# The row of s_dst: from four TensorE transposes and a ScalarE copy to a VectorE transpose and two transfers through a DRAM line

One core of a Trainium2 chip. The metric is device time in microseconds, the median of the runs of one kernel.

## The reference, cut to what matters

64 graphs of 256 nodes and 128 features go through four layers, each followed by a residual sum and a layer norm. Layer 0 is a gated recurrence of five steps. Layer 2 contains the graph attention that the change concerns:

```python
h = x @ Wp + bp
s_src = (h * a_src).sum(-1); s_dst = (h * a_dst).sum(-1)
scores = s_src[:, :, None] + s_dst[:, None, :]           # row of s_dst beside column of s_src
scores = where(scores >= 0, scores, 0.2 * scores)
attn = softmax(where(A <= 0, -inf, scores), axis=-1)
h_gat = (attn * A) @ h                                   # then layer norm, relu, a GIN layer
```

The matmul gives `s_dst` as a column (a node per partition). The scores need it as a row that every partition holds.

## The kernel before: the parts that matter

Two graphs make a pair; 32 pairs go through. A small list scheduler in the kernel places every operation of every pair in the instruction lists of five engines, from costs and latencies that it is told. `N_PAIR` limits how many pairs are in flight. The last three pairs (the tail) use a variant of the code with more TensorE transposes.

```python
N_PAIR = 8
LATENCY = {PE: 230, ACT: 80, DVE: 80, POOL: 120, SP: 1800}
# ...
ts = bank()                                               # a PSUM bank
def f():
    for c in range(C):                                    # C = 4 in a full-width pair
        nc.tensor.transpose(ts.ap[:, c * P:(c + 1) * P],
                            h2.ap[:, c, D + 1:D + 2].to_broadcast([P, P]), ident.ap)
# ... full-width pairs (29 of 32):
add(PE, 112 * C, f, [h2, ident], [ts], [ts, sd, u, mx, nm, rd])
add(ACT, act(C * P) - 45, lambda: nc.scalar.copy(sd.ap.rearrange(...), ts.ap.rearrange(...)), [ts], [sd])
# ... then on VectorE, at its place in that engine's list:
nc.vector.tensor_tensor_reduce(out=uc(c), in0=sd.ap[:, b * N:(b + 1) * N], in1=mask.ap[:, it, :], ...)
```

The column, repeated along the free dimension, is transposed against the identity: every partition of the bank gets the row. After the mask operation come leaky ReLU and exponential on ScalarE, a product and a block transpose on VectorE, four transfers of `wT`, and the weighted matmul on TensorE (L809).

A step of layer 0 is a chain as well: matmuls, tanh on ScalarE, three VectorE operations, a VectorE block transpose to `S`, four transfers of `htok`, and the next step's mixing matmul (L533), its copy and the next matmuls.

Of the kernel before, what the change touches and what calls it, by code (L numbers as in the profile page):

```python
# [7 lines left out]
F32 = mybir.dt.float32  # L8
# [4 lines left out]
P = 128  # L13
N = 256
D = 128
# [6 lines left out]
N_T = 58  # L22
N_W = 6
N_H = 6
N_PAIR = 8
N_TAIL = 3

MATS = ["w3a", "w3b", "w4a", "w4b", "w5a", "w5b", "u3", "u5",
# [11 lines left out]
PE, ACT, DVE, POOL, SP = range(5)  # L40
LATENCY = {PE: 230, ACT: 80, DVE: 80, POOL: 120, SP: 1800}


def place(p):

    return 20000 * min(p, 27) + 6000 * max(p - 27, 0)


class Buf:


    def __init__(self, tag, slots, make):
        self.tag, self.slots, self.make = tag, slots, make
        self.ap, self.slot, self.left, self.writer, self.readers = None, None, 0, [], []


class Op:
    def __init__(self, eng, cost, fn, rank, takes):
        self.eng, self.cost, self.fn, self.rank, self.takes = eng, cost, fn, rank, takes
        self.uses, self.before, self.n_before, self.ready = [], [], 0, 0  # L60


class Graph:
# [3 lines left out]
    def add(self, eng, cost, fn, rank, reads=(), writes=(), takes=()):  # L67
        op = Op(eng, cost, fn, rank, takes)
        deps = set()
        for b in reads:  # L70
            deps.update(b.writer)
            b.readers.append(op)
        for b in writes:
            deps.update(b.writer)
            deps.update(b.readers)
            b.writer, b.readers = [op], []
        for b in takes:
            b.writer = b.writer or [op]
        for b in {id(b): b for b in (*reads, *writes, *takes)}.values():
            b.left += 1  # L80
            op.uses.append(b)
        deps.discard(op)
        for d in deps:
            d.before.append(op)
        op.n_before = len(deps)
        self.ops.append(op)
        return op

    def order(self):
        clock = [0] * 5  # L90
        free = {}
        for op in self.ops:
            for b in op.takes:
                free.setdefault(b.tag, [(0, i) for i in range(b.slots)])
        waiting = [[] for _ in range(5)]
        for op in self.ops:
            if not op.n_before:
                waiting[op.eng].append(op)

        for op in reversed(self.ops):  # L100
            op.tail = op.cost + max((n.tail + (LATENCY[op.eng] if n.eng != op.eng or op.eng != PE else 0)
                                     for n in op.before), default=0)
        for op in self.ops:
            op.rank = (place(op.rank[0]) - op.tail, op.rank)
        out = []
        self.busy = [0] * 5
        while len(out) < len(self.ops):
            best = None
            for e in range(5):
                pick = None  # L110
                for op in waiting[e]:
                    at = max(op.ready, clock[e])
                    need = {}
                    for b in op.takes:
                        need[b.tag] = need.get(b.tag, 0) + 1
                    for tag, n in need.items():
                        if len(free[tag]) < n:
                            at = None
                            break
                        at = max(at, free[tag][n - 1][0])  # L120
                    if at is None:
                        continue
                    key = (at, op.rank)
                    if pick is None or key < pick[0]:
                        pick = (key, op)
                if pick is not None and (best is None or pick[0] < best[0]):
                    best = pick
            (at, _), op = best
            waiting[op.eng].remove(op)
            for b in op.takes:  # L130
                b.slot = free[b.tag].pop(0)[1]
            clock[op.eng] = at + op.cost
            self.busy[op.eng] += op.cost
            end = at + op.cost + LATENCY[op.eng]
            op.start = at
            for b in op.uses:
                b.left -= 1
                if b.left == 0 and b.slots:
                    free[b.tag].append((end, b.slot))
                    free[b.tag].sort()  # L140
            for n in op.before:
                n.n_before -= 1
                n.ready = max(n.ready, end if n.eng != op.eng or op.eng != PE else at + op.cost)
                if not n.n_before:
                    waiting[n.eng].append(n)
            out.append(op)
        self.end = max(clock)
        return out
# [9 lines left out]
def kernel(ctx: ExitStack, tc: tile.TileContext, xT, xs, adjs, mats, cols, rows, out):  # L158
    nc = tc.nc
    NPAIR = xT.shape[0]  # L160

    const = ctx.enter_context(tc.tile_pool(name="const", bufs=1))
    work = ctx.enter_context(tc.tile_pool(name="work", bufs=1))
    psum = ctx.enter_context(tc.tile_pool(name="psum", bufs=1, space=bass.MemoryType.PSUM))
    ctx.enter_context(tc.manual_schedule())
    g = Graph()

    def fixed(shape, name):
        b = Buf(name, 0, None)
        b.ap = const.tile(shape, F32, name=name)  # L170
        return b

    def temp(shape, tag, slots, name=None):
        return Buf(tag, slots, lambda i: work.tile(shape, F32, tag=f"{tag}{i}", name=name or tag))

    def flat(name):
        return temp([P, 512], "t", N_T, name)

    def wide(name):
        return temp([P, 4, D], "t", N_T, name)  # L180
# [7 lines left out]
    def bank():  # L188
        return Buf("ps", 8, lambda i: psum.tile([P, 512], F32, tag=f"ps{i}", name="ps"))


    diff, ident = fixed([P, P], "diff"), fixed([P, P], "ident")
    A = {n: fixed([P, 2, N], n) for n in ADJS[:-1]}
    aTs, a_s, aTss = A["aTs"], A["as"], A["aTss"]
# [27 lines left out]
    HT, XS = [flat("hT") for _ in range(NPAIR)], [wide("xs") for _ in range(NPAIR)]  # L222
    token = [Buf("pair", N_PAIR, lambda i: None) for _ in range(NPAIR)]

# [200 lines left out]
    maskb, ginT = fixed([P, 2, N], "maskb"), fixed([P, 2, N], "ginT")  # L425
# [50 lines left out]
    maskn, wpxn, vxn = fixed([P, 2, N], "maskn"), fixed([P, HW], "wpxn"), fixed([P, 2, D], "vxn")  # L476
# [42 lines left out]
    def build(p):  # L519
        n = [0]  # L520

        def add(eng, cost, fn, reads=(), writes=(), takes=()):
            n[0] += 1
            g.add(eng, cost, fn, (p, n[0]), reads, writes, takes)

        def mix(src, m):

# [48 lines left out]
        if p < NPAIR - N_TAIL:  # L576
            layers123(p, add, x_t, x0, (0, 1), False)
        else:
            for b in range(2):
                layers123(p, add, x_t, x0, (b,), True)  # L580

    def layers123(p, add, h, x0, bs, by_pe):

        nb = len(bs)
        C = 2 * nb
# [5 lines left out]
        def act(n, aps=0):  # L591
            return 250 + 0.745 * n + 93 * aps

        def wide(name):
            return temp([P, C, D], "t", N_T, name)

        def flat(name):
            return temp([P, C * P], "t", N_T, name)
# [118 lines left out]
        def f():  # L717
            for it in range(2):
                o, i = (b.ap.rearrange("p (b t) d -> p b t d", t=2)[:, :, it, :] for b in (xd, x_t))
                nc.scalar.activation(o, i, AF.Copy, scale=dcol.ap[:, it:it + 1])  # L720
# [13 lines left out]
        h2 = temp([P, C, HW], "h2", N_H, "h2")  # L734
# [9 lines left out]
                h2.ap[:, 2 * b:2 * b + 2, :], th.ap[:, :2 * HW].rearrange("p (t d) -> p t d", d=HW),  # L744
                hbias.ap[:, None, :].to_broadcast([P, 2, HW])), [th, hbias], [h2])

        ts = bank()

        def f():
            for c in range(C):  # L750
                nc.tensor.transpose(ts.ap[:, c * P:(c + 1) * P], h2.ap[:, c, D + 1:D + 2].to_broadcast([P, P]), ident.ap)  # L751
        u = temp([P, C * N], "w", N_W, "u") if nb == 2 else temp([P, C * N], "t", N_T, "u")
        mx, nm, rd = (temp([P, C], k, 6) for k in ("mx", "nm", "rd"))
        if by_pe:
            add(PE, 112 * C, f, [h2, ident], [ts], [ts, u, mx, nm, rd])
            sd, mask, edges = ts, maskn, A["ass"]
        else:
            sd, mask, edges = flat("sd"), maskb, a_s
            add(PE, 112 * C, f, [h2, ident], [ts], [ts, sd, u, mx, nm, rd])
            add(ACT, act(C * P) - 45, lambda: nc.scalar.copy(sd.ap.rearrange("p (c x s) -> p c x s", x=4, s=32),  # L760
                                                             ts.ap.rearrange("p (c s x) -> p c x s", x=4, s=32)),
                [ts], [sd])

        def uc(c):
            return u.ap[:, c * N:(c + 1) * N]
# [74 lines left out]
        R, o = temp([P, 2, nb, D], "t", N_T, "R"), wide("o")  # L840
        tt = [bank() for _ in range(nb)]
        v = vxn if by_pe else vx
# [96 lines left out]
```

## Time and profile before

| | before |
|---|---|
| time, median of 3 runs | 1566.67 us (1566.57 to 1567.11) |
| span of the profiled run | 1564.1 us |
| TensorE busy | 1538.2 us, 98% |
| period of a pair in the middle | 47.15 us |
| TensorE idle: first 50 us / middle / last 114 us | 6.1 / 1.8 / 18.0 us |

TensorE's records overlap, so their durations don't add up (at 593.30 us of the trace before, a group of four transposes is recorded as 0.60 us and the next matmul starts 0.44 us after it). I count as time on TensorE the distance from one start to the next. I use two figures of a trace throughout. **Work** is the count of TensorE records by form, times the median start-to-start time of that form in the trace before (429 ns for 512 columns, 216 for 256, 112 for 128 and for a transpose). **Rest** is the span less the work: waits, start and end. Before: 1564.1 = 1525.7 + 38.4.

### The profile page before, as it was taken

What the parts mean: (1) busy time and instruction counts of PE and PEld (TensorE: products, weight loads), DVE (VectorE), ACT (ScalarE), POOL (GpSimd) and SP (SyncE); (2) the same over time, 40 slices, a digit from 0 to 9 for tenths busy, and PEclk for the clock granted to TensorE, in tenths of its full rate; (3) what the DMA queues carried; (4) which work ended last, traced back from release to release, by engine and by line L of the source; (5) the groups of instructions that cost most, each with busy time, mean ns of one, the idle gap of its engine ahead of it and who ended that gap; (6) DMA issues with size and microseconds to landing.
All of it is one profiled execution on the core that took longest, in us unless ns stands there. A gap on an engine that the chain in (4) does not pass through costs nothing.

```text
span 1564.1 us, 21663 instructions
## 1 busy us (share of the span) xinstructions
PE 1538.2 (98%) x6480; PEld 1072.5 (69%) x6480; DVE 1100.4 (70%) x2550; ACT 992.3 (63%) x2227; POOL 459.5 (29%) x532
## 2 busy tenths in 40 slices
PE   8999999999999999999999999999999999999797
PEld 5556667776776676776676777666776676766686
DVE  4688787677666677666677666677666677867775
ACT  3345676666666666666676666676666667766663
POOL 0001233232333332322322333322232323323564
PEclk9999999999999999999999999999999999999998
DMA  6223454454444554444554444544445544535210
GB/s 217 43 36 54 63 75 76 75 92 77 74 68 73 90 88 75 80 65 74 93 85 74 78 69 74 95 80 77 79 70 75 95 72 84 91 53 80 40 21 28
DMA packets 719220, 117.67 MB, mean 75 GB/s; under 512 B 705408, under 2 KB 706176, under 8 KB 718976
## 3 DMA queue, kind: packets, MB, share of 16 engines
q1 hardware_dynamic: 718816, 115.76, 44.6%
q8 instruction: 53, 0.87, 0.2%
q14 instruction: 63, 0.52, 0.1%
q10 hardware_dynamic: 288, 0.53, 0.1%
HBM read 20.26 MB, written 8.39 MB: 18 GB/s over the span
## 4 chain that ended last, share of the span: by engine, by line
PE 94%; DVE 2%; POOL 1%; DMA 1%; SPq 1%; issue 0%; ACT 0%; POOLq 0%; DVEq 0%
PE ps L533 17%; PE ps L630 10%; PE ps L547 9%; PE ps L565 8%; PE ps L550 8%; PE ps L555 8%; PE ps L563 8%; PE ps L643 7%; PE ps L858 7%; PE ps L809 4%; PE ps L870 3%; PE ps L741 2%; PE ps L751 1%; SPq L514 1%; POOL rs L695 0%
## 5 line engine op out<-in xcount | busy, mean ns | idle before, releaser
L533 PE MATMUL ps<-aTs,htok 128*128 128x256 f32 x1024 | 241.5, 379 | 0.2 <-DMA htok<-S 0.2
L533 PEld LDWEIGHTS ps<-aTs,htok 128*128 128x128 f32 x1024 | 192.6, 190 | 58.6 <-issue 23.4
L569 DVE TENSOR_TENSOR hv<-hv,hT 128x512 f32<-128x512 f32 x160 | 111.1, 695 | 134.2 <-ACT hv L567 132.3
L694 POOL TENSOR_SCALAR ss<-ss 128x4 f32<-128x4 f32 (+1 forms) x105 | 31.8, 303 | 513.0 <-DVE ss L686 498.7
L536 ACT COPY mix<-ps 128x512 f32<-128x512 f32 x160 | 94.0, 587 | 131.7 <-PE ps L533 131.7
L558 ACT ACTIVATE tz<-ps,bz 128x512 f32<-128x512 f32 x160 | 109.2, 684 | 97.8 <-PE ps L555 97.3
L695 POOL TENSOR_TENSOR rs<-ss,neg_half 128x4 f32<-128x4 f32 (+1 forms) x140 | 137.7, 984 | 91.3 <-DVE ss L688 78.7
L565 PE MATMUL ps<-tr,u5h 128*128 128x512 f32 x320 | 163.6, 593 | 0.6 <-DVE tr L560 0.5
L547 PE MATMUL ps<-hT,W 128*128 128x512 f32 x320 | 163.1, 594 | 0.5 <-DMA hT<-xT_in 0.4
L550 PE MATMUL ps<-mix,w4s 128*128 128x512 f32 x320 | 162.9, 593 | 0.0
L563 PE MATMUL ps<-mix,w5s 128*128 128x512 f32 x320 | 162.9, 593 | 0.0
L555 PE MATMUL ps<-mix,dw 128*128 128x512 f32 x320 | 162.6, 593 | 0.0
L560 DVE SCALAR_TENSOR_TENSOR tr<-tr,hT 128x512 f32<-128x512 f32 x160 | 111.0, 695 | 64.1 <-ACT tr L553 63.1
L553 ACT ACTIVATE tr<-ps,br 128x512 f32<-128x512 f32 x160 | 109.1, 682 | 59.4 <-PE ps L550 59.1
L567 ACT ACTIVATE hv<-ps,bh 128x512 f32<-128x512 f32 x160 | 109.6, 685 | 47.4 <-PE ps L565 46.8
L661 POOL TENSOR_SCALAR rs<-mv 128x4 f32<-128x4 f32 (+1 forms) x70 | 34.9, 499 | 282.1 <-DVE mv L657 279.6
L570 DVE SCALAR_TENSOR_TENSOR hv<-tz,hv 128x512 f32<-128x512 f32 x160 | 108.1, 677 | 11.3 <-ACT tz L558 9.8
L572 DVE SCALAR_TENSOR_TENSOR hT<-hv,hT 128x512 f32<-128x512 f32 x160 | 112.8, 707 | 4.3 <-PE ps L858 0.5
L508 DVE STREAM_TRANSPOSE S<-hT 128x512 f32<-128x512 f32 x160 | 111.5, 698 | 1.4
L686 DVE TENSOR_REDUCE ss<-sq 128x4 f32<-128x512 f32 (+1 forms) x140 | 87.8, 633 | 25.0 <-ACT sq L683 24.8
L633 ACT COPY mix<-ps 128x512 f32<-128x512 f32 (+1 forms) x105 | 57.6, 549 | 71.1 <-PE ps L630 71.1
L743 DVE TENSOR_TENSOR h<-ps,hbias 128x260 f32<-128x260 f32 x64 | 27.2, 426 | 102.0 <-PE ps L741 101.9
(213 smaller groups left out, 3064.3 us busy)
## 6 DMA issues: line engine op xcount, KB each, us to landing
htok<-S SPq DMA_DIRECT2D x640, 64.0 KB, 2.5
xT<-S SPq DMA_DIRECT2D x232, 64.0 KB, 2.5
wT<-S SPq DMA_DIRECT2D x116, 128.0 KB, 3.8
xs<-xs_in SPq DMA_DIRECT2D x32, 256.0 KB, 2.8
hT<-xT_in SPq DMA_DIRECT2D x32, 256.0 KB, 3.0
dT<-S SPq DMA_DIRECT2D x116, 64.0 KB, 2.4
zT<-S SPq DMA_DIRECT2D x116, 64.0 KB, 2.5
y_out<-o SPq DMA_DIRECT2D x29, 256.0 KB, 2.0
```

Of the source, the lines that this page charges most:

```text
L508: lambda: nc.vector.transpose(S.ap.rearrange("p (x c r) -> p x c r", x=4, c=tiles), view(src).rearrange("p (c x s) -> p x c s", x=4, c=til ...
L533: nc.tensor.matmul(t.ap[:, b * N:(b + 1) * N], src.ap[:, 2 * b + j, :], m.ap[:, j, :], start=(j == 0), stop=(j == 1))
L547: add(PE, 865, lambda tg=tg: nc.tensor.matmul(tg.ap, mat("u3"), hT.ap, start=True, stop=False, skip_group_check=True), [hT, W0], [tg], [tg ...
L550: add(PE, 865, lambda tg=tg, mT=mT: nc.tensor.matmul(tg.ap, w4s.ap, mT.ap, start=False, stop=False, skip_group_check=True), [mT, w4s], [tg])
L555: add(PE, 865, lambda tg=tg, mT=mT: nc.tensor.matmul(tg.ap, dw.ap, mT.ap, start=False, stop=True, skip_group_check=True), [mT, dw], [tg])
L560: add(DVE, 735, lambda tr=tr: nc.vector.scalar_tensor_tensor(tr.ap, tr.ap, 1.0, hT.ap, op0=ALU.add, op1=ALU.mult), [hT], [tr])
L563: add(PE, 865, lambda tv=tv, mT=mT: nc.tensor.matmul(tv.ap, w5s.ap, mT.ap, start=True, stop=False), [mT, w5s], [tv], [tv, hv])
L565: add(PE, 865, lambda tv=tv, tr=tr: nc.tensor.matmul(tv.ap, u5h.ap, tr.ap, start=False, stop=True), [tr, u5h], [tv])
L569: add(DVE, 735, lambda hv=hv: nc.vector.tensor_sub(hv.ap, hv.ap, hT.ap), [hT], [hv])
L572: add(DVE, 735, lambda hv=hv: nc.vector.scalar_tensor_tensor(hT.ap, hv.ap, 0.5, hT.ap, op0=ALU.mult, op1=ALU.add), [hv], [hT])
L630: nc.tensor.matmul(t.ap[:, b * N:(b + 1) * N], src.ap[:, 2 * b + j, :], m.ap[:, j, :], start=(j == 0), stop=(j == 1))
L695: nc.gpsimd.tensor_tensor(rs.ap, ss.ap, neg_half.ap[:, :C], op=ALU.pow)
```

## The change

Its intent: take the row's transposes off TensorE, the engine that bounds. VectorE transposes the repeated column in 32x32 blocks, as in layer 0, where each of 160 such transposes goes with four transfers that bring the blocks to their places (640 of `htok` in the trace). After it four partitions, the ones that the program reads, hold a quarter of each block's row. A transfer scatters these four 512-byte rows in 32-byte pieces to a DRAM line, and another reads the line into all partitions. The scheduler is told of the long latency, and two more pairs may be in flight. The tail keeps its transposes.

```diff
-N_PAIR = 8
+N_PAIR = 10
 ...
-            sd, mask, edges = flat("sd"), maskb, a_s
-            add(PE, 112 * C, f, [h2, ident], [ts], [ts, sd, u, mx, nm, rd])
-            add(ACT, act(C * P) - 45, lambda: nc.scalar.copy(...), [ts], [sd])
+            mask, edges = maskb, a_s
+            quarter, sd = temp([P, C, 4, 8], "quarter", 4), flat("sd")
+            line = Buf("line", 8, lambda i: dram.tile([1, C * P], F32, ...))
+            add(DVE, 300, lambda: nc.vector.transpose(quarter.ap.rearrange("p c x v -> p c v x"),
+                                                      h2.ap[:, :, D + 1:D + 2].to_broadcast([P, C, 32])),
+                [h2], [quarter], [quarter])
+            add(SP, 650, lambda: nc.sync.dma_start(line.ap.rearrange("o (f q v) -> (o q) f v", q=4, v=8),
+                                                   quarter.ap[0:P:32].rearrange("q c x v -> q (c x) v")),
+                [quarter], [line], [line], lat=4000)
+            add(SP, 430, lambda: nc.sync.dma_start(sd.ap, line.ap.to_broadcast([P, C * P])), [line], [sd],
+                [sd, u, mx, nm, rd], lat=3500)
```

(The scheduler reads `op.lat` in place of `LATENCY[op.eng]`; the tail's branch is moved, not changed.)

More of the change, by code (lines that the diff above doesn't have):

```diff
@@ L59, in __init__ @@
         self.eng, self.cost, self.fn, self.rank, self.takes = eng, cost, fn, rank, takes
-        self.uses, self.before, self.n_before, self.ready = [], [], 0, 0
+        self.uses, self.before, self.n_before, self.ready, self.lat = [], [], 0, 0, LATENCY[eng]
 class Graph:
@@ L100, in order @@
         for op in reversed(self.ops):
-            op.tail = op.cost + max((n.tail + (LATENCY[op.eng] if n.eng != op.eng or op.eng != PE else 0)
+            op.tail = op.cost + max((n.tail + (op.lat if n.eng != op.eng or op.eng != PE else 0)
                                      for n in op.before), default=0)
@@ L133, in order @@
             self.busy[op.eng] += op.cost
-            end = at + op.cost + LATENCY[op.eng]
+            end = at + op.cost + op.lat
             op.start = at
@@ L163 @@
     work = ctx.enter_context(tc.tile_pool(name="work", bufs=1))
+    dram = ctx.enter_context(tc.tile_pool(name="dram", bufs=1, space=bass.MemoryType.DRAM))
     psum = ctx.enter_context(tc.tile_pool(name="psum", bufs=1, space=bass.MemoryType.PSUM))
@@ L520, in build, with add @@
         n = [0]
-        def add(eng, cost, fn, reads=(), writes=(), takes=()):
+        def add(eng, cost, fn, reads=(), writes=(), takes=(), lat=None):
             n[0] += 1
-            g.add(eng, cost, fn, (p, n[0]), reads, writes, takes)
+            op = g.add(eng, cost, fn, (p, n[0]), reads, writes, takes)
+            op.lat = lat or LATENCY[eng]
         def mix(src, m):
@@ L745, in layers123 @@
                 hbias.ap[:, None, :].to_broadcast([P, 2, HW])), [th, hbias], [h2])
-        ts = bank()
-        def f():
-            for c in range(C):
-                nc.tensor.transpose(ts.ap[:, c * P:(c + 1) * P], h2.ap[:, c, D + 1:D + 2].to_broadcast([P, P]), ident.ap)
         u = temp([P, C * N], "w", N_W, "u") if nb == 2 else temp([P, C * N], "t", N_T, "u")
@@ L754, in layers123, with f @@
         if by_pe:
-            add(PE, 112 * C, f, [h2, ident], [ts], [ts, u, mx, nm, rd])
-            sd, mask, edges = ts, maskn, A["ass"]
-        else:
-            sd, mask, edges = flat("sd"), maskb, a_s
-            add(PE, 112 * C, f, [h2, ident], [ts], [ts, sd, u, mx, nm, rd])
-            add(ACT, act(C * P) - 45, lambda: nc.scalar.copy(sd.ap.rearrange("p (c x s) -> p c x s", x=4, s=32),
-                                                             ts.ap.rearrange("p (c s x) -> p c x s", x=4, s=32)),
-                [ts], [sd])
+            sd, mask, edges = bank(), maskn, A["ass"]
+            def f():
+                for c in range(C):
+                    nc.tensor.transpose(sd.ap[:, c * P:(c + 1) * P], h2.ap[:, c, D + 1:D + 2].to_broadcast([P, P]),
+                                        ident.ap)
+            add(PE, 112 * C, f, [h2, ident], [sd], [sd, u, mx, nm, rd])
+        else:
+            mask, edges = maskb, a_s
+            quarter, sd = temp([P, C, 4, 8], "quarter", 4), flat("sd")
+            line = Buf("line", 8, lambda i: dram.tile([1, C * P], F32, tag=f"line{i}", name="line"))
+            add(DVE, 300, lambda: nc.vector.transpose(quarter.ap.rearrange("p c x v -> p c v x"),
[6 more added lines that the diff above has]
+                [sd, u, mx, nm, rd], lat=3500)
         def uc(c):
```

## The prediction

> **What bounds the kernel now.** I read the first page of the profile from the top. Busy time by engine comes first:
>
> ```profile
> span 1564.1 us, 21663 instructions
> PE 1538.2 (98%) x6480; PEld 1072.5 (69%) x6480; DVE 1100.4 (70%) x2550; ACT 992.3 (63%) x2227; POOL 459.5 (29%) x532
> ```
>
> TensorE is busy 98% of the span, and the next engine only 70%. Busy is not yet "bound", so I asked for busy time by stretch (columns: stretch, length, then each engine's busy microseconds, granted TensorE clock, DMA share, GB/s):
>
> ```profile
> 0.00:50.00 50.00, 43.86 (x128) 26.25 (x129) 21.15 (x43) 17.56 (x26) 0.83 (x7) 1.00 0.60 179
> 50.00:200.00 150.00, 149.14 (x538) 92.24 (x537) 119.05 (x277) 81.25 (x159) 18.43 (x19) 1.00 0.35 51
> 200.00:1300.00 1100.00, 1099.48 (x4628) 766.31 (x4627) 767.91 (x1728) 728.79 (x1634) 332.93 (x353) 1.00 0.48 78
> 1300.00:1450.00 150.00, 149.57 (x637) 104.45 (x636) 111.35 (x245) 100.84 (x233) 46.56 (x51) 1.00 0.49 78
> 1450.00:1564.10 114.10, 96.11 (x555) 83.29 (x553) 80.90 (x261) 63.89 (x179) 60.76 (x102) 0.93 0.14 29
> ```
>
> Of the 25.9 us in which TensorE has nothing (1564.1 - 1538.2), 6.1 lie in the first 50 us and 18.0 in the last 114; in the 1400 us between it idles 1.8 us in all. The waits of TensorE agree, the largest being these (engine and line, what it waited for, total, times, longest):
>
> ```profile
> PE ps L630 <- DVE x_t L667: 6.6, 2, 5.4
> PE ps L533 <- DMA aTs<-adjs_in: 6.1, 1, 6.1
> PE ps L630 <- ACT hg L818: 2.9, 1, 2.9
> ```
>
> The second is the first load of the run, the other two lie in the last 114 us. In the middle the program repeats one pair of graphs after another with a period of 47.15 us (the projection of line 643 comes at 509.11, 556.26 and 603.40 in the chain that ended last), and TensorE is busy in all 47.15. So there, **a microsecond of TensorE work taken out of every pair is a microsecond of period, and nothing else shortens it.**
>
> [...] The trace has 273 ns for one record of the group removed. But records overlap, as the sum below shows. [...] each VectorE transpose of an L508 tile is followed by four transfers that put the blocks where they belong. [...] The trace has 2.5 us from issue to landing for the 64 KB pieces and 2.8 for 256 KB loads. [...] the read of the line carries the write's semaphore. No trace of the kernel before has such a pair.
>
> **The change part by part.** It concerns the 29 pairs that go in full width (32 pairs less a tail of 3; the tail keeps its transposes).
>
> Removed from TensorE: four transposes per pair, 116 in all. Their cost is read from starts, not durations:
>
> ```profile
> 592.44 1.03 PE L870 MATMUL ps<-R,pw 128*128 128x256 f32 x4
> 593.30 0.60 PE L751 MATMUL ps<-ident,h 128*128 128x128 f32 x4
> 593.74 0.59 PE L550 MATMUL ps<-mix,w4s 128*128 128x512 f32 x1
> ```
>
> The group is shown as 0.60 us, but the next matmul starts 0.44 us after it (0.43 at 640.45, 687.69 and, with 0.44, at 546.16). 29 x 0.433 = **12.6 us**, all of it in the stretch without idle time. (The 19.3 us of busy time of line 751 counts overlap and the tail, and would be 50% too much.)
>
> Removed from ScalarE: the copies, all 29:
>
> ```profile
> L760 ACT COPY sd<-ps 128x512 f32<-128x512 f32 x29 | 17.0, 586 | 21.0 <-PE ps L751 20.9
> ```
>
> 17.0 us of an engine busy 63%: nothing on the path. One PSUM bank per pair is freed for the time from transposes to copy: no TensorE wait for a bank shows above, so nothing.
>
> Added to VectorE: one 32x32 transpose with 128 elements per partition. From
>
> ```profile
> L508 DVE STREAM_TRANSPOSE S<-hT 128x512 f32<-128x512 f32 x160 | 111.5, 698 | 1.4
> L508 DVE STREAM_TRANSPOSE S<-u 128x1024 f32<-128x1024 f32 x29 | 35.9, 1239 | 0.0
> ```
>
> the slope is (1239 - 698) / 512 = 1.06 ns per element, the fixed part 157 ns, so some 292 ns (estimate) x 29 = 8.5 us. VectorE is busy 32.8 of a 47.15 us period, and goes to 33.1: beside TensorE's work.
>
> Added to the queue of SyncE: two issues per pair, one scattering four partitions in pieces of 32 bytes, one reading 256 KB. Four issues take 2.65 us in the timeline, so 0.66 each: 2 x 0.66 = 1.3 us per pair on top of about 28 (43 issues a pair: 20 of htok, 8 of xT, 4 each of wT, dT and zT, two loads, a store). Bytes: 29 x 256 KB = 7.6 MB on 117.67, hence DMA share from 0.49 to about 0.51.
>
> Latency from the column (h2) to the row (sd). Before: 0.43 of transposes, 0.59 of copy, and places in queues. After: 0.3 + issue 0.66 + about 2.4 landing, queue, issue 0.66 + about 2.8 landing, at least 6.8 us. Whether it is covered is a matter of order. The built programs' instruction order tells: counting the TensorE work between the last matmul of h2 and the first weighted matmul of the same pair (line 809 before) with this trace's start-to-start times (0.22 us per 128-column matmul, 0.43 per 256, 0.86 per 512), a steady pair has 38 us before and 60 after; the first pair 25 and 41. The scheduler was told of the latency and the limit of pairs in flight rises from 8 to 10, so it put other pairs' work in between. 22 us more room for some 6 us more latency, and up to 12 other transfers between (12 x 0.66 = 8 us).
>
> The order's ends: the first 232 TensorE matmuls are in the same order in both programs, and so are the last 397 (beyond the last 114 us), as are the last 317 VectorE and 118 GpSimd instructions. So the 18 us idle at the end and the 6.1 at the start should stay.
>
> Sum: -12.6 (TensorE) + 0 (ScalarE, VectorE, queue, hidden) + 0 to 2 for small waits of a reordered middle = **about -12.5: 1566.67 to 1554.2 us, -0.8%.**
>
> **Rivals.** *One: the row comes late and VectorE, which runs in order, stands at the mask operation (L770).* Its wait for sd before is only 4.5 us in all. For it: two dependent transfers, one with 32-byte pieces, and every microsecond that reaches TensorE costs 29. Against it: the 60 us above, and VectorE's 30% of free time absorbs a microsecond or two. If it came: 1 us a pair makes 1583, and gain and loss cancel at 0.43.
> *Two: the read of the line waits at the head of SyncE's queue and holds the htok transfers behind it.* For it: the queue is in order and the read waits there for the write. Against it: in the order 26 of 29 pairs have 8 or 12 other transfers between write and read (5 us or more against a landing near 2.4), one has 4, and only the first and last have none. Those two could hold the queue 2 to 3 us each, with 41 us of TensorE work in hand: 0 to 3 us in total, to 1557.
> *Three: the reordering itself matters more than the removed work.* Nearly every line of the middle moves. It cannot gain much: only 1.8 us of idle time is there. It can lose, if chains now stand too close. The distance between successive steps of one pair in TensorE work is 28 to 38 us in the steady part (11 to 40 before), and its least, 10.3, is the same in both: no sign of it. I allow up to 5 us.
> *Four: the transfers are slowed by the new ones.* 58 on 1326, 7.6 MB on 117.67, DMA engines half idle: nothing.
>
> **Range and chances.** The low end, 1551, is the sum plus 3 us of luck in the tail, where the granted clock is 0.93 and waits of up to 5 us stand. The high end, 1559, is rivals two and three with some 5 us together. Faster by over 2% needs 31 us, two and a half times all the work removed: 0.01. Slower by over 2% needs rival one at 1.5 us a pair (12.6 + 31.3 over 29): 0.02. Within 2%: 0.97.
>
> **What would show each step right or wrong.** TensorE busy near 1525.6 us and 6364 records; the period 46.7 us with TensorE busy throughout. Right for the latency: no TensorE wait in the middle, VectorE's waits for sd from a transfer below some 10 us in total. VectorE's busy time up by 8 to 9, ScalarE's down by 17, neither seen in the span. Line write and row read each landing in 2 to 3.5 us. Rival one: waits of L770's successor for sd of over 0.4 us a pair, with TensorE idle in the middle. Rival two: SyncE's queue waiting for the write in many pairs. Rival three: TensorE idle between 200 and 1400 us, ended by other releasers. A gain over 16 us would mean that the transposes cost TensorE more than their start-to-start time.

The sum is -12.6 us for TensorE, 0 for ScalarE, VectorE and queue, and 0 to 2 us for small waits, put together as about -12.5, or 1554.2 us. The landings of about 2.4 and 2.8 us are estimates after the trace before: 2.4 to 2.5 us for its 64 KB pieces, 2.8 for its 256 KB loads of `xs`. That VectorE and the queue run in order was assumed there.

## The result

| | before | changed |
|---|---|---|
| time, median of 4 runs | 1566.62 us (1565.65 to 1567.11) | 1553.53 us (1551.42 to 1556.00) |
| span of the profiled run = work + rest | 1564.1 = 1525.7 + 38.4 | 1551.2 = 1512.7 + 38.5 |
| TensorE records | 6480 | 6364 |
| period in the middle | 47.15 us | 46.70 us |

The ratio is 0.9918 (95%: 0.9901 to 0.9935): 0.8% faster. Ratios here are the mean time of one kernel's fast runs over that of the other's fast runs of the same rounds, so not quite the ratio of the medians quoted.

The changed kernel's page, span and busy time by engine:

```profile
span 1551.2 us, 21563 instructions
PE 1522.9 (98%) x6364; PEld 1060.9 (68%) x6364; DVE 1106.7 (71%) x2579; ACT 972.0 (63%) x2198; POOL 487.1 (31%) x532
```

TensorE is still the bound: 116 records fewer, 98% as before. The changed kernel by stretch, columns as in the prediction (stretch, length, busy microseconds by engine, granted TensorE clock, DMA share, GB/s):

```profile
0.00:50.00 50.00, 44.10 (x128) 26.41 (x129) 21.15 (x43) 17.57 (x26) 0.83 (x7) 1.00 0.65 200
50.00:200.00 150.00, 149.91 (x533) 92.81 (x532) 119.28 (x286) 80.04 (x156) 20.66 (x21) 1.00 0.36 54
200.00:1300.00 1100.00, 1098.92 (x4578) 764.64 (x4577) 777.85 (x1749) 713.80 (x1614) 358.68 (x351) 1.00 0.51 85
1300.00:1450.00 150.00, 146.99 (x622) 103.35 (x622) 114.79 (x264) 103.22 (x241) 50.78 (x61) 1.00 0.48 76
1450.00:1551.20 101.20, 82.98 (x509) 73.67 (x508) 73.59 (x240) 57.32 (x164) 56.15 (x94) 0.93 0.12 27
```

TensorE's idle time is 5.9 us at the start, 18.2 in the last stretch and 4.2 in the middle (1.8 before). A whole period of each kernel in the middle, before and then changed, in the same view:

```profile
509.11:556.26 47.15, 47.15 (x201) 32.86 (x200) 32.77 (x75) 31.39 (x71) 14.34 (x15) 1.00 0.49 79
```

```profile
620.85:667.55 46.70, 46.70 (x195) 32.49 (x195) 32.49 (x76) 30.53 (x70) 15.43 (x15) 1.00 0.51 86
```

TensorE is busy all of it in both, and the period is 0.45 us shorter: four transposes at 112 ns. The waits of TensorE in the changed kernel (engine and line, what it waited for, total, times, longest) name the row nowhere:

```profile
PE ps L632 <- DVE x_t L669: 6.6, 2, 5.4
PE ps L535 <- DMA aTs<-adjs_in: 5.9, 1, 5.9
PE ps L567 <- DVE tr L562: 3.0, 2, 1.9
PE ps L632 <- ACT hg L828: 2.9, 1, 2.9
```

The three long ones are those of the kernel before, at the start and in the tail. The third is new. Line numbers of the changed kernel are higher by a few: its L535, L562, L567, L632 and L780 are L533, L560, L565, L630 and L770 before. VectorE's two groups of the new path (line, operation, tiles, forms, count, busy, mean ns, idle time just before and what ended most of it):

```profile
L780 DVE CUSTOM_DVE_ANT_0 u<-sd,maskb 128x256 f32<-128x256 f32 x116 | 47.3, 463 | 23.3 <-DMA sd<-line 23.2
L765 DVE STREAM_TRANSPOSE quarter<-h 128x128 f32<-128x128 f32 x29 | 10.8, 373 | 0.1
```

VectorE does stand for the row, 23.2 us in all (8 of 29 pairs). Six of its seven long stands (3.3 to 3.9 us) lie in the steady periods, with no TensorE wait after them. The seventh, in one of the last full-width pairs, comes through, as the timeline at 1299 us shows (start, length, engine, line; in brackets the idle time before it and what ended it):

```profile
1299.17 1.33 DVE L780 CUSTOM_DVE_ANT_0 u<-sd,maskb 128x256 f32<-128x256 f32 x1 [2.05 <-DMA sd<-line]
1301.86 0.68 DVE L562 SCALAR_TENSOR_TENSOR tr<-tr,hT 128x512 f32<-128x512 f32 x1
1302.60 0.70 PE L567 MATMUL ps<-tr,u5h 128*128 128x512 f32 x1 [1.95 <-DVE tr L562]
```

VectorE stands 2.05 us for the row at the mask operation, the product of L562 comes behind it in VectorE's order, and TensorE waits 1.95 us for that product. The `tr` that ScalarE gives to the product (L555) was done at 1298.36 us, while VectorE stood, and yet the product started behind the mask operations, at 1301.86. In e0 the same place shows 1.55 and 1.60 us. The other 1.1 us of the third wait lie at 1382 us, where VectorE is merely busy. From the completion times of the transfers in the trace, counted from the start of their issue, the write of the line lands after 1.80 us (median of 29, 1.74 to 2.77) and the row after 3.53 us (3.00 to 4.86). In the first and the last pair SyncE's queue stands 1.2 us for the write before it issues the read (at 147.99 us in the first).

### The profile page after: what moved, and what is told of

It reads as the page before. It is cut to its first block, busy times and chain, and to the rows that moved or that the text cites. A ratio compares the mean times of both kernels' runs of the same rounds, so it can differ in the third digit from the quotient of the medians.

```text
span 1551.2 us, 21563 instructions
## 1 busy us (share of the span) xinstructions
PE 1522.9 (98%) x6364; PEld 1060.9 (68%) x6364; DVE 1106.7 (71%) x2579; ACT 972.0 (63%) x2198; POOL 487.1 (31%) x532
## 4 chain that ended last, share of the span: by engine, by line
PE 94%; DVE 2%; POOL 1%; DMA 1%; SPq 1%; issue 0%; ACT 0%; POOLq 0%; DVEq 0%
PE ps L535 18%; PE ps L632 10%; PE ps L567 9%; PE ps L549 9%; PE ps L557 9%; PE ps L565 9%; PE ps L552 9%; PE ps L645 7%; PE ps L868 7%; PE ps L819 3%; PE ps L880 3%; PE ps L743 2%; SPq L515 1%; DMA sd<-line 1%; DVE u L780 0%; POOL rs L697 0%
## 5 line engine op out<-in xcount | busy, mean ns | idle before, releaser
L697 POOL TENSOR_TENSOR rs<-ss,neg_half 128x4 f32<-128x4 f32 (+1 forms) x140 | 155.5, 1111 | 518.6 <-DVE ss L690 509.9
L535 PE MATMUL ps<-aTs,htok 128*128 128x256 f32 x1024 | 242.3, 380 | 0.7 <-DMA htok<-S 0.5
L535 PEld LDWEIGHTS ps<-aTs,htok 128*128 128x128 f32 x1024 | 194.2, 190 | 62.5 <-issue 31.8
L567 PE MATMUL ps<-tr,u5h 128*128 128x512 f32 x320 | 163.4, 593 | 3.1 <-DVE tr L562 3.0
L555 ACT ACTIVATE tr<-ps,br 128x512 f32<-128x512 f32 x160 | 109.0, 681 | 81.4 <-PE ps L552 76.3
L565 PE MATMUL ps<-mix,w5s 128*128 128x512 f32 x320 | 159.9, 593 | 0.0
L549 PE MATMUL ps<-hT,W 128*128 128x512 f32 x320 | 159.4, 593 | 0.0
L562 DVE SCALAR_TENSOR_TENSOR tr<-tr,hT 128x512 f32<-128x512 f32 x160 | 111.6, 698 | 44.2 <-ACT tr L555 43.5
L572 DVE SCALAR_TENSOR_TENSOR hv<-tz,hv 128x512 f32<-128x512 f32 x160 | 115.7, 723 | 35.2 <-ACT tz L560 33.7
L560 ACT ACTIVATE tz<-ps,bz 128x512 f32<-128x512 f32 x160 | 109.9, 688 | 30.5 <-PE ps L557 30.1
L574 DVE SCALAR_TENSOR_TENSOR hT<-hv,hT 128x512 f32<-128x512 f32 x160 | 116.4, 728 | 2.2
L552 PEld LDWEIGHTS ps<-mix,w4s 128*128 128x128 f32 x320 | 60.3, 190 | 54.3 <-issue 45.1
L645 PEld LDWEIGHTS ps<-W,mix 128*128 128x128 f32 x512 | 74.6, 192 | 28.2 <-issue 25.3
L663 POOL TENSOR_SCALAR rs<-mv 128x4 f32<-128x4 f32 (+1 forms) x70 | 31.1, 444 | 189.4 <-DVE mv L659 187.0
```

Of the source, the lines that this page charges most:

```text
L535: nc.tensor.matmul(t.ap[:, b * N:(b + 1) * N], src.ap[:, 2 * b + j, :], m.ap[:, j, :], start=(j == 0), stop=(j == 1))
L549: add(PE, 865, lambda tg=tg: nc.tensor.matmul(tg.ap, mat("u3"), hT.ap, start=True, stop=False, skip_group_check=True), [hT, W0], [tg], [tg ...
L552: add(PE, 865, lambda tg=tg, mT=mT: nc.tensor.matmul(tg.ap, w4s.ap, mT.ap, start=False, stop=False, skip_group_check=True), [mT, w4s], [tg])
L562: add(DVE, 735, lambda tr=tr: nc.vector.scalar_tensor_tensor(tr.ap, tr.ap, 1.0, hT.ap, op0=ALU.add, op1=ALU.mult), [hT], [tr])
L565: add(PE, 865, lambda tv=tv, mT=mT: nc.tensor.matmul(tv.ap, w5s.ap, mT.ap, start=True, stop=False), [mT, w5s], [tv], [tv, hv])
L567: add(PE, 865, lambda tv=tv, tr=tr: nc.tensor.matmul(tv.ap, u5h.ap, tr.ap, start=False, stop=True), [tr, u5h], [tv])
```

## The experiments

The theory is that the gain is TensorE time taken out of a stretch that TensorE bounds, and that the order hides the longer way to the row. Its rivals: the gain comes from the freed ScalarE, the freed bank or the new order; or the latency is hidden by something other than what the order provides. "Room" below is the TensorE work that the built program's instruction order puts between two dependent points, counted with the start-to-start times. Room of the row: from the last matmul of h2 to the weighted matmul of the same pair. Room of a step: from the last matmul of one step of a pair to the first that needs the next step's mix. I give the steady value of both, for the second the least step of a steady pair; the first pair has 12.9 in every run. The row's values differ by a microsecond or so from the prediction's, where one form of matmul was undercounted. The prediction's distance of steps is another measure, from start to start, so its least, 10.3, is not to be compared with this column.

| run | median us | ratio to before | work + rest, us | room of row | room of step |
|---|---|---|---|---|---|
| before | 1564.9 to 1565.8 | 1 | 1525.7 + 38.4 | 39 | 17 |
| changed (e0) | 1552.8 | 0.9917 | 1512.7 + 39.1 | 61 | 21 |
| e4: transposes put back | 1563.4 | 0.9989 | 1525.7 + 35.9 | 62 | 21 |
| e6: ScalarE copy put back | 1551.1 | 0.9915 | 1512.7 + 36.4 | 61 | as changed |
| e5: before, transposes doubled | 1584.6 | 1.0121 | 1538.6 + 45.2 | 35 | 16 |
| e1: before, 10 pairs | 1566.9 | 1.0007 | 1525.7 + 41.3 | 37 | 22 |
| e2: changed, 8 pairs | 1611.1 | 1.0288 | 1512.7 + 97.8 | 58 | 12 |
| e14: changed, 9 pairs | 1557.8 | 0.9956 | 1512.7 + 45.0 | 61 | 21 |
| e3: general latency told | 1560.4 | 0.9967 | 1512.7 + 45.8 | 50 | 23 |
| e9: almost no latency told | 1616.2 | 1.0325 | 1512.7 + 99.8 | 36 | 21 |
| e13: e9, row not read | 1549.0 | 0.9900 | 1512.7 + 33.9 | 36 | 21 |
| e7: one more hop, told | 1560.9 | 0.9979 | 1512.7 + 47.6 | 70 | 25 |

### Putting the transposes back (e4)

```diff
+            ts = bank()
+            def spare():
+                for c in range(C):
+                    nc.tensor.transpose(ts.ap[:, c * P:(c + 1) * P], h2.ap[:, c, D + 1:D + 2].to_broadcast([P, P]), ident.ap)
+            add(PE, 112 * C, spare, [h2, ident], [ts], [ts])
```

> The changed kernel with its four transposes a pair put back into a spare bank that nobody reads; everything else of the change stays (VectorE transpose, line write, row read, 10 pairs, no ScalarE copy). Theory (the gain is TensorE time taken out of a stretch that TensorE bounds): all of the gain goes, 1566 us (1564 to 1568), period back from 46.70 to 47.14 us, TensorE without waits in the middle. Rival (the gain comes from the freed bank, the freed ScalarE or the new order): it keeps at least half of the gain, 1560 us or less.

1563.4 us, 10.6 more than the changed kernel (e0 ran on another chip; the kernel before differs by 0.9 us between the two). One period of it:

```profile
529.18:576.32 47.14, 47.14 (x199) 32.90 (x199) 33.06 (x75) 31.83 (x74) 14.06 (x15) 1.00 0.41 70
```

The period is back at 47.14 with TensorE busy throughout, and the work back at 1525.7. The median is 0.6 us below the range that I gave: the rest came out some 3 us smaller than in the changed kernel. e4 takes a bank again, and keeps ScalarE free and the new order. So **the gain in the middle is the transposes' time on TensorE and nothing else.** Of the run as a whole nearly all is given back: against the kernel before the ratio is 0.9989 (95%: 0.9977 to 1.0001).

### Putting the copy back (e6), with the changed kernel beside it (e0)

```diff
+            junk = flat("junk")
+            add(ACT, act(C * P) - 45, lambda: nc.scalar.copy(junk.ap, h2.ap.rearrange("p c d -> p (c d)")[:, :C * P]),
+                [h2], [junk], [junk])
```

> The changed kernel itself, once more, beside the other runs of this call: 1553.5 us within 2.5 us. It is here so that the putting-back and copying-back runs have the changed kernel in the same rounds.

> The changed kernel with a ScalarE copy of 512 columns per full-width pair put back, into a buffer that nobody reads (29 x 0.586 us = 17 us of ScalarE). Theory (ScalarE's copy lay beside TensorE's work): no change, within 2.5 us of the changed kernel in the same rounds. Rival (the gain, or a part of it, is ScalarE's freed time): 4 us or more slower.

The changed kernel repeats at 1552.8 us, and with the copy it takes 1551.1, within the spread of single runs. ScalarE's 17 us were worth nothing.

### Doubling the transposes in the kernel before (e5)

```diff
             add(PE, 112 * C, f, [h2, ident], [ts], [ts, sd, u, mx, nm, rd])
+            add(PE, 112 * C, f, [h2, ident], [ts])
```

> The kernel before with the four transposes of each full-width pair done twice into the same bank (8 in place of 4), 116 more. Theory (a group costs TensorE its start-to-start time of 0.433 us in a stretch without idle time): 29 x 0.433 = 12.6 us slower than before, within 2.5. If the record's 0.60 us were the cost: 17.3 us. Rival (transposes are absorbed by slack): under 5 us.

The run took 1584.6 us, 19.7 more by the medians: a miss against 12.6. The work rose by 12.9 (116 x 112 ns), as the theory has it. The other 6.8 us are rest. The order became another one, and in it TensorE waits for a later pair's load (`PE ps L533 <- DMA xs<-xs_in` 2.8 us in 7 waits) and starts mixing matmuls (L533) late after the last matmul of a step (L565), 7.2 us in all from start to start. Its room of a step is 15.6 us in place of 17.4, which would fit, but no run tests it. So the time alone can't tell 112 ns from the 150 of the record (0.60 / 4); the start-to-start times and e4 do.

### More pairs alone (e1), fewer pairs with the change (e2, e14)

```diff
-N_PAIR = 8        # e1: the kernel before          -N_PAIR = 10      # e2, e14: the changed kernel
+N_PAIR = 10                                        +N_PAIR = 8  (e2)   /   9  (e14)
```

> The kernel before with the limit of pairs in flight raised from 8 to 10, its transposes kept. Theory: the middle has no idle time to win, so the same as before, 1566.6 us within 2 us. Rival (the reordering that the limit allows is what gained): half of the gain or more, 1560 us or less.

> The changed kernel with the limit of pairs put back to 8. In its instruction order some 58 us of TensorE work still lie between h2 and the weighted matmul of the same pair (61 with 10). Theory: the row is in time with 8 as well, 1553.5 us within 3 us. Rival (10 pairs are needed to cover the two transfers): TensorE waits in the middle, half the gain or more lost, 1560 us or more.

> The changed kernel with a limit of 9 pairs. In its instruction order at least 20.8 us of TensorE work lie between the last matmul of one step of a pair and the first that needs the next step's tokens' mix, as with 10 pairs; with 8, which lost 58 us, it is 12.2. Theory (the 8-pair order fails because the longer way to the row takes its time out of the steps, when pairs are too few to fill it): 1553 us within 3. Rival (more pairs help in some other way, gradually): between the two, 1570 to 1590 us.

Ten pairs give the kernel before nothing (its six runs fall into two groups, near 1564 and near 1569 us, with the kernel before at 1565.8). Eight pairs cost the changed kernel 58 us: it would have been 2.9% slower than before. The theory's expectation for e2 was wrong, because it looked at the room of the row alone. The row is in time there: VectorE waits for it 3.9 us in the whole run. TensorE stands elsewhere:

```profile
PE ps L535 <- DMA htok<-S: 29.3, 36, 1.6
PE ps L535 <- DMA aTs<-adjs_in: 5.9, 1, 5.9
PE ps L567 <- DVE tr L562: 5.7, 14, 1.2
```

36 waits are for the tokens of the next step of layer 0: 29.3 of the 59 us that the rest grew by. What remains is spread over shorter waits. With the row's way 20 us longer, a pair stays in flight longer. Eight pairs can't fill the time, so the scheduler drew the steps together: 12.2 us of room in place of 17. Such a step needs about 10.3 us at the least, an estimate from durations in the profile: tanh 0.69, three VectorE operations and a transpose 2.8, four issues 2.65, the last landing 1.8 after its issue, mixing 1.73, copy 0.59, with nothing queued anywhere. 12.2 leaves 2 us for waiting in the lists of five engines, and by this reading it isn't enough. No run changes the room of a step alone, so the reading is argued and not shown.

With 9 pairs the rooms are those of the changed kernel and the period is 46.70 again. The run is 5 us slower than the changed kernel, 1.8 us outside the range, and no pair in the middle accounts for it: the rest differs from 1300 us on (TensorE busy 145.4 of the 150 us to 1450, against 147.0) and by small waits. Some of it may be the granted clock: its mean over the profiled run is 0.995 in e14 (and in e3 and e7) and 0.996 in the changed kernel, and 0.001 of 1557.6 us is 1.6 us (an estimate; the rounding leaves 0 to 3).

### What the scheduler is told (e3, e9), and which wait it is (e13)

```diff
-                [quarter], [line], [line], lat=4000)      # e3: no lat (1800)    e9, e13: lat=80
-                [sd, u, mx, nm, rd], lat=3500)            # e3: no lat (1800)    e9, e13: lat=80
# e13 only: the mask operation reads a constant buffer
-                    out=uc(c), in0=sd.ap[:, b * N:(b + 1) * N], ...
+                    out=uc(c), in0=(sd if by_pe else BLIND[0]).ap[:, b * N:(b + 1) * N], ...
```

> The changed kernel, but the scheduler uses its general latency of 1.8 us for both transfers in place of 4.0 and 3.5. Measured in the changed kernel, from the end of the issue the write takes some 1.2 us and the read 3.0: the general figure is enough for the write and 1.2 us short for the read, 0.6 us in sum too generous. The order leaves 50 us of TensorE work between h2 and the weighted matmul (61 in the changed kernel, 36 in the near one that lost) and at least 21 us between the steps of one pair (12 in the 8-pair one that lost). Theory (what matters is that the order's room is about the true latency, with enough pairs): 1551 to 1557 us. Rival (the special latencies of 4.0 and 3.5 are needed): 1565 us or more.

> The changed kernel, but the scheduler is told 80 ns instead of 4000 and 3500 for the latencies of the two transfers: the order then has no transfer between write and read in 28 of 29 pairs, and 36 us of TensorE work between h2 and the weighted matmul in place of 61. From the changed kernel's landings (write 1.8 us, row 3.5 us from issue) the row comes some 4 us later than the order has it. Rival one of the prediction, provoked: VectorE waits 3 to 5 us a pair for the row (some 110 us in all), SyncE's queue about 1.2 us a pair for the write. If the room that the scheduler left is what hides the transfers: TensorE waits in the middle and half the gain or more is lost, 1560 us or more, up to 1600. If free time of VectorE (some 13 us a pair) absorbs it anyway: VectorE's waits are seen but TensorE stays busy, 1553 to 1557 us.

> The near kernel (1616 us) in its own instruction order, but the mask operations of VectorE read a constant buffer in place of the row, so that VectorE has nothing to wait for; both transfers are still made, and SyncE's queue still holds the read until the write has landed. The result is wrong on purpose. It tells apart why the near order loses. If VectorE standing at the mask operation for the row (105.6 us of waits in the near run) is the cause: most of the loss goes, 1575 us or less. If the held queue of SyncE (15.8 us of waits for the write between 500 and 1200 us) or the order itself is the cause: it stays, 1600 us or more.

The near order, e9, loses 63 us against the changed kernel, and at 1616.2 us lies beyond the 1600 that I gave as the most. VectorE's waits for the row in it:

```profile
DVE u L780 <- DMA sd<-line: 105.6, 29, 4.7
```

And the two largest waits of TensorE in it:

```profile
PE ps L535 <- DMA htok<-S: 28.5, 13, 3.2
PE ps L567 <- DVE tr L562: 14.2, 14, 2.6
```

In all 29 pairs VectorE stands at the mask operation, 3.6 us on average. The block transposes of other pairs that come behind it in VectorE's order are late, and TensorE waits for their tokens. The granted TensorE clock was lower too: 0.66 in each of three stretches of 5 us, from 588, 687 and 882 us, and 0.988 as the mean of the run, against 0.996 in the changed kernel. By an estimate that is some 13 of the 63 us (0.008 of 1612.5 us). Which waits bring the clock down is not shown.

e13 has the same instruction order on every engine (VectorE has one memset more), the same transfers, and SyncE's queue still waits for the write (15.8 us in 14 times between 500 and 1200 us, as in e9). Only VectorE doesn't wait. It takes 1549.0 us, and its steady periods are 46.70:

```profile
700.00:793.40 93.40, 93.40 (x390) 64.94 (x389) 66.53 (x150) 61.32 (x138) 27.20 (x30) 1.00 0.50 85
```

TensorE is busy in all of two periods. So the loss of e9 is **VectorE's stand for the row**; neither the order nor the held queue makes it by itself. (Its result is wrong by construction. It still passed the comparison, so the tolerance doesn't see this row, and a pass says nothing of the new way to it.) Its 1549.0 us suggests what a quicker row could still bring to the changed kernel: about 4 us. The order is another one, so this is no bound; but the wait of L567 that the row caused in the changed kernel is gone in e13.

In between lies e3, and it corrects both theories. (The sum in its expectation has the wrong sign: 0.6 us too much for the write and 1.2 too little for the read make 0.6 too little.) VectorE waits almost as long there as in e9:

```profile
DVE u L780 <- DMA sd<-line: 88.8, 27, 6.4
```

Yet most of its periods in the middle are 46.70 to 47.1, and it loses 7.5 us in all, not 63. With 50 us of room nearly the same stand of VectorE is nearly covered, with 36 it isn't. The two orders differ in more than this room, so that it is the room which decides is argued, not shown.

### One more hop (e7)

```diff
+            line2 = Buf("line2", 8, ...)
+            add(SP, 650, lambda: nc.sync.dma_start(line2.ap, line.ap), [line], [line2], [line2], lat=4000)
-            add(SP, 430, lambda: nc.sync.dma_start(sd.ap, line.ap.to_broadcast([P, C * P])), [line], [sd],
+            add(SP, 430, lambda: nc.sync.dma_start(sd.ap, line2.ap.to_broadcast([P, C * P])), [line2], [sd],
```

> The changed kernel with one more hop: the line is copied to a second DRAM line by one more transfer, and the row is read from that; the scheduler is told (4.0 us for it), 10 pairs. The row comes some 2 us later plus a place in the queue; the order leaves 70 us of TensorE work in place of 61 and at least 25 us between steps. Theory (latency that the order knows of, with pairs enough to fill it, costs nothing): 1553 us within 4, period 46.7. Rival (latency costs in itself): 2 us for each pair, 1600 us or more.

1560.9 us: 8 us slower than the changed kernel, outside my range, though far from 2 us a pair (an estimate; the write of the line was measured at 1.80 us). Periods alternate between 46.70 and 46.87, and VectorE waits for the row 1.4 us in all. The remaining microseconds lie in the first pairs and in the last 300 us, as with e3 and e14. Apart from the granted clock told of with e14, what in the order of the ends makes 5 to 8 us there stays open; I didn't test it. No version that computes the right result clearly beats the changed kernel (e6's 1551.1 is within its spread).

## Why the prediction was right, and where it wasn't

It said 1554.2 us (1551 to 1559) and the time is 1553.53.

- **TensorE, -12.6 us.** Right in cause and size: 13.0 by work (116 x 112 ns), and e4 gives it back. Reading starts in place of durations was the step that mattered: with 0.60 us a group it would have been 17.4. TensorE's busy time fell further than forecast, to 1522.9 us and not 1525.6, because its idle time rose by 2.4 (4.2 us in the middle, where no wait was expected).
- **ScalarE, -17 us, worth nothing.** Right (e6). Its busy time fell by 20.3.
- **VectorE, some 292 ns more a pair.** Measured 364 ns (median), so 10.6 us and not 8.5, beside TensorE's work all the same. VectorE's whole busy time rose by 6.3, below the 8 to 9 given as a sign; why isn't known.
- **Latency.** The write was thought to land after about 2.4 us and does after 1.8; the row after about 2.8 and does after 3.5. The sum, 5.3, is right by luck: the write, 2 KB in 64 pieces of 32 bytes, was quicker than the 64 KB pieces of `htok` in the same run (2.45 us), and the row, a line of 2 KB read into 128 partitions, slower than the plain 256 KB loads (3.04 and 3.12 us). The 6.8 us for the whole way count each issue twice, because these landings are counted from the start of the issue: transpose, write and read measure 0.36 + 1.80 + 3.53 = 5.7, without queues.
- **VectorE's wait for the row below some 10 us.** Wrong: 23.2 us. In the steady periods it didn't reach TensorE; at 1299 us one stand of 2.05 did, for 1.95.
- **Rival one: "1 us a pair makes 1583".** The coefficient is wrong. 3.1 us a pair of VectorE's time (88.8 over 29, e3) cost 7.5 us in all, while 3.6 (e9) cost 63. So a wait of VectorE was not by itself a wait of TensorE: it became one through what stood behind it in the order. In the steady periods it was rightly dismissed; once, at 1299 us, it came.
- **Room.** The conclusion was right, but the prediction named the told latency and the 10 pairs in one breath and counted mainly the room of the row. e2 shows that this count is blind to half of the danger: 58 us of room and a loss of 58 us. The count to make is the room of every chain that shares the engines. The prediction did look at the distance of steps, from start to start, but didn't ask what 8 pairs would do to it.
- **Rival two, the held queue.** Rightly dismissed: in the changed kernel SyncE waits 2.4 us for the write, in the two pairs named, and e13 bears 15.8 us of it.
- **The ends.** 18.0 and 6.1 us of idle time became 18.2 and 5.9: right. That the rest stayed as it was (38.4 and 38.5) has some luck in it: idle time rose by 2.4 us in all, while the time at a granted clock of 0.50 before the last matmul fell from 13.7 to 10.2 us, worth 1.7 (an estimate: half of it; four transposes take 0.85 us in such a stretch, at 1486.84 us of the trace before, and 0.43 beside it, at 1490.23).

## What to carry to other kernels

Here one engine was busy in every microsecond of a period, and a saving on it was worth its start-to-start time (four transposes at 112 ns, 0.45 us a period), but only while the other chains kept their room (12 us between steps in e2 went with a loss of 58 us); e5 shows that the order the scheduler makes anew can add half as much again. The trade of engine time for latency was paid with work in flight, so scheduler latency, buffer limits and the new path belong in one change: here the same edit is 0.8% faster with 10 pairs and the latency told, 2.9% slower with 8 pairs, and 3.3% slower with almost no latency told. Check the room of all the chains, not only of the one that was changed.
